# A decoder layer on one core: the quarter of the down projection that is multiplied directly moves from the end to both ends, and GpSimd issues the loads of the hidden operands

## The chip, the core and the metric

The kernel runs on one core of a Trainium2 chip as one launch. The metric is the device time of one execution in microseconds; the median of three runs of the kernel before is 2515.79 us (2514.77 to 2517.98).

## What is computed

Eight sequences of 100 tokens, model width 1024, go through a post-norm decoder layer: decayed linear attention, attention over a context of 722 tokens and the sequence itself, and a gated feed-forward block. Each is added to its input and normalised over the width. Only the last block matters here:

```python
gate = jnp.einsum('bsd,hd->bsh', x, w_gate)      # 4096 hidden rows
up = jnp.einsum('bsd,hd->bsh', x, w_up)
gated = jax.nn.silu(gate) * up
y = jnp.einsum('bsh,dh->bsd', gated, w_down)     # the down projection
out = _layernorm(x + y)
```

All of it is float32.

## The kernel before

**Numbers in two parts.** TensorE multiplies a fast 32-bit type, so every operand is split into a high part (ScalarE casts it, `split2`, L67) and a low rest (VectorE subtracts, L68). A product is three matmuls (`mm3`, L86 to L88): high by high, high by low, low by high. Activations lie transposed, width on the 128 partitions and tokens along the free side, in two halves of N = 400 tokens.

**Seven products instead of eight.** A unit of gate, up or down is a two by two block product. `seven` (L342 to L406) does it with seven products of 12 matmuls (128x128 weights by 128x400) instead of eight: four weight blocks a11 to a22 are loaded as two raw tiles `wst` (`load_raw`, three buffers, SP queue), VectorE makes three mixed blocks of them (L375 to L378), ScalarE and VectorE split the mixed and the raw blocks into `w` (four buffers) and `wd` (one buffer), and the products use seven operands b11, b21, t2, t3, t1, t4, b22 that hold blocks of the activations and their differences. `in_turn` (L408) interleaves neighbouring units by product, and a scheduler with its own model of time then fixes the order of the instructions on every engine and queue. Each engine works strictly in that order.

**Gate and up.** There are 16 units of 256 hidden rows. `combine` (L859 to L879) turns the product of gate and up of one unit into the operands of the down projection and stores them in device memory: for a seven-product quarter seven operands with their rests in `hd` (four stores, 1400, 200, 400 and 800 KB), for the direct quarter the four blocks alone in `h3d` (two stores of 800 KB). One quarter is four units. Tiles `r`, `t` and `h` of `combine` have one buffer each, so the next unit writes them only when the stores of the one before have landed.

**Down.** The hidden rows are summed in four quarters. Quarters 0, 1 and 2 are done by `seven`: four units each, whose products are added by VectorE straight to the rows `y` of the result (L360, L369). Quarter 3 is done directly: `proj` (L100) makes one product of 24 matmuls for each of the eight 128-wide blocks m of the result and for each half of the tokens, and VectorE adds it to `y` (L994). So the direct quarter comes last, first all eight blocks of half 0 and then all eight of half 1. Its eight split weight tiles `ws` are made once in half 0 and kept for half 1 (four in `w`, four in operand slots that are free by then).

**Operand slots.** Ten slots of 1600 KB take the operands of the down projection in rotation: `f`, three `z`, four `big` (which until the end of the up projection hold the operands of gate and up) and two `h` (which lie where pools of gate and up lay). `load_chunk` (L918) loads the seven operands of a quarter, one DMA of 1600 KB each. These DMAs are issued by SP, on the same queue as the weights `wst` and the stores, where the scheduler has put them. So a weight load stands behind an operand load that waits for its slot, and behind its bytes.

**The end.** Half 0 is normalised (`norm_root`, `scaled`) while half 1 is multiplied. Half 1 uses `norm_early`: the mean over the first six blocks (L294) is taken off before the last two are there, then `norm_more` and `norm_late` correct it. `scaled` (L271) and the stores of the result (L274) end the kernel.

Of the kernel before, what the change touches and what calls it, by code (L numbers as in the profile page):

```python
# [11 lines left out]
ALU = mybir.AluOpType  # L12
# [8 lines left out]
KT = D // P  # L21
QT = KT // 2
# [11 lines left out]
UNITS = NHID // 2  # L34
# [5 lines left out]
def decoder_layer(ctx, tc, xT, cT, w1, wo1, w2, wo2, wc, w3, wd, gw, qw, kw, trig, dec, mask, out):  # L40
    nc = tc.nc

    def sbuf(name, bufs, side=None):
        return tc.tile_pool(name=name, bufs=bufs, side=side, reuse_waits="tile")
# [11 lines left out]
    def f32(ap):  # L56
        return ap.bitcast(F32)
# [38 lines left out]
    def acc_tag():  # L96
        turn[0] += 1
        return "as"[turn[0] % 2]

    def proj(w, z, n=N, tag="a"):  # L100
        acc = bank(tag)[:, :n]
        for k in range(KT):
            t = z[k // QT]
            mmw(acc, w, k, t[:, 0, k % QT, :n], t[:, 1, k % QT, :n], k == 0, k == KT - 1)
        return acc
# [54 lines left out]
    hd = dr.tile([QT - 1, 7, P, 2, QT, N], FR, name="hd")  # L160
    h3d = dr.tile([4, P, 2, QT, N], FR, name="h3d")
# [129 lines left out]
    def norm_early(y, s1, p, first=KT - 1):  # L291
        n = y.shape[2]
        mean = bank("s")[:, :n]
        nc.tensor.matmul(mean, onem7, s1, start=True, stop=True)  # L294
        f = (KT - 1) / first
        for m in range(first):
            nc.vector.scalar_tensor_tensor(y[:, m], mean, -f, y[:, m], ALU.mult, ALU.add)
        var, delta = bank("v")[:, :n], bank("s")[:, :n]
        nc.tensor.matmul(var, onem, squares(y, p, range(first)), start=True, stop=False, skip_group_check=True)
        return mean, var, f, delta, first  # L300
# [26 lines left out]
    def load_raw(src):  # L327
        st = wp.tile([P, KT * P], F32, tag="wst", name="wst", bufs=3)
        if isinstance(src, list):
            for i, s in enumerate(src):  # L330
                nc.sync.dma_start(out=st[:, i * H:(i + 1) * H].rearrange("p (u c) -> p u c", u=QT), in_=s)
        else:
            nc.sync.dma_start(out=st, in_=src)
        return st

    def w_split(src, w=None):
        if w is None:
            w = wp.tile([P, 2, KT * P], FR, tag="w", name="w", bufs=4)
        split(w, src)
        return w  # L340
# [67 lines left out]
    def in_turn(units):  # L408

        at = sorted((7 * i + 2 * j, i) for i in range(len(units)) for j in range(-1, 7))  # L410
        started = {}
        for _, i in at:
            make, then = units[i]
            if i not in started:
                started[i] = make()
            try:
                next(started[i])
            except StopIteration:
                then()


    with sbuf("l1", 2) as p:
# [106 lines left out]
        for blk in range(2):  # L529
            w = load_w(w1[0, 2 + blk])  # L530
# [12 lines left out]
        def unit(h, i, then):  # L543
            c = {}
            return (lambda: seven(p, w1[h, i], w1[h, i + 1], zb, "ass", temp, c.__setitem__),
                    lambda: then(h, [(hb, c[name]) for hb, name in zip(HB, C)]))
# [75 lines left out]
    early = []  # L622
    with sbuf("l2", 2) as p:
        for kv in range(NKV):
            for i0, i1 in ((0, 4), (4, 6)) if kv == 0 else ((0, 2), (2, 4), (4, 6)):
                if (kv, i0) == (0, 4):
                    load_context(0)
                ws = [load_w(w2[kv, i]) for i in range(i0, i1)]
# [5 lines left out]
                for half in range(2):  # L634
                    bs = slice(half * NB, (half + 1) * NB)
                    for i in range(i0, i1):
                        acc = proj(ws[i - i0], z1[half], tag=acc_tag())
# [139 lines left out]

    fp = ctx.enter_context(sbuf("fp", 1, "right"))  # L780
    z2p = ctx.enter_context(sbuf("z2", 1, "right"))
    zb = {}
# [76 lines left out]
    def combine(u, r):  # L859
        h = ff.tile([P, 7, N], FR, tag="h", name="h")  # L860
        q, j = u // QT, u % QT
        if q == QT - 1:
            split2(h[:, 0:4], r, r)
            nc.sync.dma_start(out=f32(h3d[:, :, 0, j]).rearrange("c p n -> p c n"), in_=f32(h[:, 0:4]))
            nc.sync.dma_start(out=f32(h3d[:, :, 1, j]).rearrange("c p n -> p c n"), in_=r)
            return
        t = ff.tile([P, 4, N], F32, tag="t", name="t")
        pairs = r.rearrange("p (i x) n -> p i x n", x=2)
        nc.vector.tensor_tensor(t[:, 0:2], pairs[:, :, 1], r[:, 0:2], ALU.subtract)
        nc.vector.tensor_tensor(t[:, 2], r[:, 3], t[:, 0], ALU.subtract)  # L870
        nc.vector.tensor_tensor(t[:, 3], r[:, 2], t[:, 2], ALU.subtract)
        split2(h[:, 3:7], t, t)
        split2(h[:, 1:3], r[:, 2:4], r[:, 2:4])
        split2(h[:, 0], r[:, 0], r[:, 0])
        to = lambda a, b, l: f32(hd[q, a:b, :, l, j]).rearrange("c p n -> p c n")
        nc.sync.dma_start(out=to(0, 7, 0), in_=f32(h))
        nc.sync.dma_start(out=to(0, 1, 1), in_=r[:, 0:1])
        nc.sync.dma_start(out=to(1, 3, 1), in_=r[:, 2:4])
        nc.sync.dma_start(out=to(3, 7, 1), in_=t)  # L879
# [13 lines left out]

    def after_up(u):
        if u == QT:
            load_chunk(0, down_order[:1])
        elif u == UNITS - 2:
            load_y(fp)
        elif u == UNITS - 1:
            ffpool.__exit__(None, None, None)  # L900
            sppool.__exit__(None, None, None)
            load_y(ctx.enter_context(sbuf("yy", 1)))
            pools.append(sbuf("hk", 1))
            hk = pools[0].__enter__()
            hk_slots.append(lambda: hk.tile([P, 2, QT, N], FR, tag="h", name="h", bufs=2))
            slots[0:0] = hk_slots * 2


    slots = [f_tile, z_tile, z_tile] + [lambda: big([P, 2, QT, N])] * 4 + [z_tile]
# [4 lines left out]
    def next_slot():  # L914
        slots.append(slots.pop(0))
        return slots[-1]()

    def load_chunk(q, names):  # L918
        for name in names:
            chunk[q, name] = next_slot()  # L920
            nc.sync.dma_start(out=f32(chunk[q, name]), in_=f32(hd[q, ORDER7.index(name)]))

    def load_y(pool):
        for _ in range(2):
# [15 lines left out]
    def down_w(q, m):  # L940


        w = wd[q * QT:(q + 1) * QT, m // QT].rearrange("u p c -> p u c")
        c = m % QT * 2 * P
        return [w[:, :, c + i * P:c + (i + 1) * P] for i in range(2)]

    def down_unit(q, m):
        def make():
            if m == 0 and q == 0:
                load_chunk(0, down_order[1:])  # L950
            z = {name: chunk[q, name] for name in ORDER7}
            into = {"c%d%d" % (i + 1, j + 1): y2[m // 2][:, i, j * N:(j + 1) * N] for i in range(2) for j in range(2)}
            return seven(fp, down_w(q, m), down_w(q, m + 1), z, "ass", into=into)

        def then():
            if m != 2:
                return
            if q < QT - 2:
                load_chunk(q + 1, down_order)
            else:  # L960
                for half in range(2):
                    z3.append([next_slot() for _ in range(2)])
                    for i in range(2):
                        nc.sync.dma_start(out=f32(z3[half][i]), in_=f32(h3d[2 * i + half]))
        return make, then

    for name in C:
        gated_block(0, name, None)
    z3 = []
    in_turn([unit(u) for u in range(1, UNITS) for unit in (gate_unit, up_unit)]  # L970
            + [down_unit(q, m) for q in range(QT - 1) for m in range(0, KT, 2)])
    pools[0].__exit__(None, None, None)
    slots = [slot for slot in slots if slot not in hk_slots]


    ln_exp()
    with sbuf("ln3", 2, "right") as lnp:
        ws = []
        for half in range(2):
            y = rows(half)  # L980
            s1 = lnp.tile([P, N], F32, tag="s1", name="s1", bufs=2)
            early = None
            for m in range(KT):
                if half == 0:
                    w = None
                    if m >= QT:
                        w = next_slot().rearrange("p l k n -> p l (k n)")[:, :, :KT * P]
                    ws.append(w_split(load_raw(down_w(QT - 1, m)), w))
                elif m == KT - 2:
                    early = norm_early(y, s1, lnp, m)  # L990
                acc = proj(ws[m], z3[half], tag=acc_tag())
                if early:
                    nc.vector.scalar_tensor_tensor(y[:, m], early[0], -early[2], y[:, m], ALU.mult, ALU.add)
                nc.vector.tensor_tensor(y[:, m], y[:, m], acc, ALU.add)  # L994
                if early:
                    norm_more(y, early, lnp, m)
                else:
                    add_up(s1, y, m)
            dst = lambda m, half=half: out[:, m, half * N:(half + 1) * N]
            if half == 0:  # L1000
                scaled(y, norm_root(y, s1, lnp), dst)
            else:
                norm_late(y, early, lnp, dst)
# [71 lines left out]
```

## Time and profile before

| what | value |
|---|---|
| median of three runs | 2515.79 us |
| the profiled execution: its own time | 2517.7 us |
| its span, first to last instruction | 2515.9 us |
| TensorE busy | 2465.4 us, 98 % of the span |
| VectorE busy | 1992.2 us, 79 % |
| ScalarE busy | 1343.5 us, 53 % |
| GpSimd busy | 481.2 us, 19 %; nothing after 1700 us |
| mean granted TensorE clock | 0.993 |
| moved by DMA | 433.96 MB, mean 172 GB/s |

The span is cut by instructions, so the profiled execution's own time is 1.8 us above it, and it is 1.9 us above the median of the runs. TensorE is the engine to look at: matmuls of 128x400 follow each other every 0.18 us, and time is lost where they don't. "Idle" of another engine costs nothing by itself. Times in the views are microseconds from the start of the span; the down projection runs from about 2220 us to the end.

### The profile page before, as it was taken

The page shows a single profiled execution, that of the slowest core. Times are in us where ns is not written, and L with a number is a line of the kernel's source. Part 1 is how long each engine was busy: PE and PEld are TensorE (multiplying, and loading weights), DVE is VectorE, ACT ScalarE, POOL GpSimd, SP SyncE. Part 2 cuts the span into 40 slices and gives each one's busy share as a digit, 9 for nine tenths or more (in the row PEclk, how much of TensorE's full clock was granted, in tenths as well). Part 3 has the DMA queues.
Part 4 walks back from the last instruction along what each step waited for, and adds up shares of the span by engine and source line. Part 5 has one row for each costly group of instructions (what it writes and reads, how often), then busy time and mean ns, then how long its engine had stood idle before and what let it go on. Part 6 is the DMA issues. An engine that isn't in the chain of part 4 may idle for free.

```text
span 2515.9 us, 37158 instructions
## 1 busy us (share of the span) xinstructions
PE 2465.4 (98%) x14036; PEld 2442.0 (97%) x14036; DVE 1992.2 (79%) x3110; ACT 1343.5 (53%) x2264; POOL 481.2 (19%) x234
## 2 busy tenths in 40 slices
PE   8999999999899999999999999999999999999997
PEld 8999999999899999999999999999999999998997
DVE  7678876568989798899999999866987777666656
ACT  6667676335767565556566566533544544432221
POOL 0111111002645334433433433100000000000000
PEclk9999999999999999999999999999999999999999
DMA  7334445774444654554554554574455445388731
GB/s 240 110 110 127 136 144 187 239 266 148 144 152 133 207 175 142 178 166 151 169 176 144 166 192 135 189 273 152 145 181 192 159 160 167 127 302 311 250 102 53
DMA packets 224450, 433.96 MB, mean 172 GB/s; under 512 B 47338, under 2 KB 168042, under 8 KB 211854
## 3 DMA queue, kind: packets, MB, share of 16 engines
q1 hardware_dynamic: 223118, 427.39, 50.7%
q0 software_dynamic: 1152, 4.19, 1.1%
q8 instruction: 110, 1.80, 0.3%
q14 instruction: 70, 0.57, 0.1%
HBM read 322.18 MB, written 109.35 MB: 172 GB/s over the span
## 4 chain that ended last, share of the span: by engine, by line
PE 89%; DVE 6%; ACT 1%; DMA 1%; issue 1%; SPq 0%; DVEq 0%; ACTq 0%
PE a L88 18%; PE a L86 18%; PE a L87 18%; PE s L88 9%; PE s L87 9%; PE s L86 9%; PE v L88 2%; PE v L86 2%; PE v L87 2%; PE s L491 1%; PE s L688 1%; DVE r L120 1%; DVE r L119 1%; PE s L148 1%; DMA tp<-in_xT 1%
## 5 line engine op out<-in xcount | busy, mean ns | idle before, releaser
L86 PE MATMUL a<-big,w 128*128 128x400 f32 (+2 forms) x1808 | 611.4, 339 | 11.7 <-ACT big L67 7.4
L87 PE MATMUL a<-big,w 128*128 128x400 f32 (+2 forms) x1808 | 611.1, 338 | 0.0
L88 PE MATMUL a<-big,w 128*128 128x400 f32 (+2 forms) x1808 | 609.7, 338 | 0.0
L67 ACT CAST w<-wst 128x1024 fp32r<-128x1024 f32 (+1 forms) x231 | 239.2, 1038 | 389.4 <-PE s L88 130.7
L68 DVE TENSOR_TENSOR w<-wst,w 128x1024 fp32r<-128x1024 f32 (+1 forms) x231 | 281.0, 1218 | 117.0 <-ACT w L67 115.1
L86 PEld LDWEIGHTS a<-big,w 128*128 128x128 f32 x1808 | 341.3, 189 | 13.3 <-ACT big L67 7.7
L87 PEld LDWEIGHTS a<-big,w 128*128 128x128 f32 x1808 | 342.0, 189 | 1.3 <-DVE big L68 0.3
L88 PEld LDWEIGHTS a<-big,w 128*128 128x128 f32 x1808 | 342.0, 189 | 0.9 <-DVE w L68 0.2
L86 PE MATMUL s<-big,w 128*128 128x400 f32 x664 | 230.6, 347 | 0.1
L87 PE MATMUL s<-big,w 128*128 128x400 f32 x664 | 229.2, 345 | 0.0
L88 PE MATMUL s<-big,w 128*128 128x400 f32 x664 | 229.1, 346 | 0.0
L125 POOL PARTITION_ALL_REDUCE ss<-sq x56 | 161.1, 2881 | 336.3 <-DMA zd<-y 167.0
L605 POOL PARTITION_ALL_REDUCE kss<-ksq x64 | 173.2, 2706 | 116.4 <-ACT ksq L604 115.7
L86 PE MATMUL a<-z,w 128*128 128x400 f32 x488 | 168.6, 346 | 8.0 <-ACT r L118 4.3
L88 PE MATMUL a<-z,w 128*128 128x400 f32 x488 | 169.4, 348 | 0.7 <-DVE w L68 0.7
L87 PE MATMUL a<-z,w 128*128 128x400 f32 x488 | 169.4, 347 | 0.0
L87 PE MATMUL s<-z,w 128*128 128x400 f32 x400 | 139.1, 348 | 2.4 <-DVE z L68 2.4
L86 PE MATMUL s<-z,w 128*128 128x400 f32 x400 | 139.9, 350 | 0.0
L88 PE MATMUL s<-z,w 128*128 128x400 f32 x400 | 139.4, 348 | 0.0
L722 ACT ACTIVATE s<-s,rk 128x400 f32<-128x400 f32 x160 | 87.7, 591 | 91.9 <-DVE sm L742 65.5
L86 PEld LDWEIGHTS s<-big,w 128*128 128x128 f32 x664 | 124.6, 188 | 1.4 <-ACT w L67 0.4
L87 PEld LDWEIGHTS s<-big,w 128*128 128x128 f32 x664 | 124.6, 188 | 1.1
(330 smaller groups left out, 5650.9 us busy)
## 6 DMA issues: line engine op xcount, KB each, us to landing
wst<-in_w SPq DMA_DIRECT2D x135, 512.0 KB
w<-wcd SPq DMA_DIRECT2D x64, 1024.0 KB
wst<-in_wo SPq DMA_DIRECT2D x64, 512.0 KB
hd<-h SPq DMA_DIRECT2D x12, 1400.0 KB
wst<-in_wd SPq DMA_DIRECT2D x64, 256.0 KB
big<-o1d SPq DMA_DIRECT2D x16, 800.0 KB
qd<-d SPq DMA_DIRECT2D x32, 400.0 KB
q<-qd SPq DMA_DIRECT2D x32, 400.0 KB
```

Source lines behind the costliest of these rows:

```text
L67: nc.scalar.copy(hi, src)
L68: nc.vector.tensor_tensor(lo, src, f32(hi), ALU.subtract)
L86: nc.tensor.matmul(acc, lh, rh, start=start, stop=False, skip_group_check=chain)
L87: nc.tensor.matmul(acc, lh, rl, start=False, stop=False, skip_group_check=chain)
L88: nc.tensor.matmul(acc, ll, rh, start=False, stop=stop, skip_group_check=chain)
L119: nc.vector.scalar_tensor_tensor(q, ss, eps, q, ALU.add, ALU.mult)
L120: nc.vector.scalar_tensor_tensor(q, q, 3.0, r, ALU.subtract, ALU.mult)
L125: nc.gpsimd.partition_all_reduce(y, x, P, op)
L148: nc.tensor.transpose(tr[0:T, b * P:(b + 1) * P], vt[:, b * T:(b + 1) * T], ident)
L491: nc.tensor.matmul(bt(o)[:, b], vv[:, b * P:(b + 1) * P], pf[:, b], start=True, stop=True)
L605: nc.gpsimd.partition_all_reduce(ss[:, at], sq[:, at], P, RED.add)
L722: nc.scalar.activation(sc, sp, AF.Copy, scale=rk[:, c:c + 1])
```

## The change

- The direct quarter is now quarter 0, the first that gate and up produce. `combine` stores units 0 to 3 to `h3d` and units 4 to 15 to `hd` (index q - 1).
- Half 0 of the direct quarter is multiplied right after the last up unit: eight products of 24 matmuls, each added to `y`. It needs two operand tiles; the first is loaded after unit 4, the second when its slot is free. During these eight products the seven operands of quarter 1 are loaded, one load put into the program before each.
- Then follow quarters 1, 2 and 3 by `seven`, with twelve units in one `in_turn` as before, but separate from gate and up.
- Half 1 of the direct quarter comes last. Its weights are loaded and split again, since the first split is not kept (eight more loads of 512 KB, eight more casts, eight more subtractions).
- Half 0 is normalised while half 1 of the direct quarter is multiplied.
- All 25 loads of down operands, 21 by `load_chunk` and four of `h3d`, 1600 KB each, are now issued by GpSimd, on its own queue; before all of them were SP's.
- The order of the slots differs: the two `h` slots come in ahead of the last one.

```diff
 def combine(u, r):
-        if q == QT - 1:
+        if q == 0:
...
-        to = lambda a, b, l: f32(hd[q, a:b, :, l, j]).rearrange("c p n -> p c n")
+        to = lambda a, b, l: f32(hd[q - 1, a:b, :, l, j]).rearrange("c p n -> p c n")
...
         if u == QT:
-            load_chunk(0, down_order[:1])
+            load_direct(0, 1)
...
-            slots[0:0] = hk_slots * 2
+            slots[-1:-1] = hk_slots * 2
...
-            nc.sync.dma_start(out=f32(chunk[q, name]), in_=f32(hd[q, ORDER7.index(name)]))
+            nc.gpsimd.dma_start(out=f32(chunk[q, name]), in_=f32(hd[q - 1, ORDER7.index(name)]))
+
+    def load_direct(half, blocks=2):
+
+        for i in range(len(z3[half]), blocks):
+            z3[half].append(next_slot())
+            nc.gpsimd.dma_start(out=f32(z3[half][i]), in_=f32(h3d[2 * i + half]))
...
+            if m == 2:
+                if q < QT - 1:
+                    load_chunk(q + 1, down_order)
+                else:
+                    load_direct(1)
...
-    in_turn([unit(u) for u in range(1, UNITS) for unit in (gate_unit, up_unit)]
-            + [down_unit(q, m) for q in range(QT - 1) for m in range(0, KT, 2)])
+    z3 = [[], []]
+    in_turn([unit(u) for u in range(1, UNITS) for unit in (gate_unit, up_unit)])
+
+    def direct(half, m, w=None):
+        return proj(w_split(load_raw(down_w(0, m)), w), z3[half], tag=acc_tag())
+
+    load_direct(0)
+    for m in range(KT):
+        load_chunk(1, down_order[m:m + 1])
+        y = rows(0)
+        nc.vector.tensor_tensor(y[:, m], y[:, m], direct(0, m), ALU.add)
+    in_turn([down_unit(q, m) for q in range(1, QT) for m in range(0, KT, 2)])
...
             for m in range(KT):
-                if half == 0:
+                if half == 1:
+                    if m == KT - 2:
+                        early = norm_early(y, s1, lnp, m)
+                        f = early[2]
                     w = None
                     if m >= QT:
                         w = next_slot().rearrange("p l k n -> p l (k n)")[:, :, :KT * P]
-                    ws.append(w_split(load_raw(down_w(QT - 1, m)), w))
-                elif m == KT - 2:
-                    early = norm_early(y, s1, lnp, m)
-                acc = proj(ws[m], z3[half], tag=acc_tag())
-                if early:
-                    nc.vector.scalar_tensor_tensor(y[:, m], early[0], -early[2], y[:, m], ALU.mult, ALU.add)
-                nc.vector.tensor_tensor(y[:, m], y[:, m], acc, ALU.add)
+                    acc = direct(half, m, w)
+                    if early:
+                        nc.vector.scalar_tensor_tensor(y[:, m], early[0], -f, y[:, m], ALU.mult, ALU.add)
+                    nc.vector.tensor_tensor(y[:, m], y[:, m], acc, ALU.add)
```

More of the change, by code (lines that the diff above doesn't have):

```diff
@@ L948, in make @@
         def make():
-            if m == 0 and q == 0:
-                load_chunk(0, down_order[1:])
             z = {name: chunk[q, name] for name in ORDER7}
@@ L955, in then @@
         def then():
[L956 to L964, printed above, removed]
+            if m == 2:
[3 more added lines that the diff above has]
+                    load_direct(1)
         return make, then
@@ L968, in decoder_layer @@
         gated_block(0, name, None)
-    z3 = []
-    in_turn([unit(u) for u in range(1, UNITS) for unit in (gate_unit, up_unit)]
-            + [down_unit(q, m) for q in range(QT - 1) for m in range(0, KT, 2)])
+    z3 = [[], []]
[8 more added lines that the diff above has]
+    in_turn([down_unit(q, m) for q in range(1, QT) for m in range(0, KT, 2)])
     pools[0].__exit__(None, None, None)
@@ L977, in decoder_layer @@
     with sbuf("ln3", 2, "right") as lnp:
-        ws = []
         for half in range(2):
```

## The prediction

> **What bounds the kernel now.** I read the busy shares, the windows by stage, the waits of TensorE, the chain that ended last, then VectorE's timeline and the DMA packets at the places that these name. TensorE is busy 98 % of the span, so only stretches with fewer matmuls than its pace hold anything to win. Windows of 50 us of the down projection, columns: TensorE busy and matmuls in brackets, then weight loads, VectorE, ScalarE, GpSimd, granted clock, DMA share, GB/s:
>
> ```profile
> 2200.00:2250.00 50.00, 50.00 (x276) 50.00 (x275) 35.79 (x49) 19.21 (x24) 0.00 (x0) 1.00 0.80 295
> 2250.00:2300.00 50.00, 48.95 (x263) 47.25 (x263) 31.06 (x46) 11.02 (x13) 0.00 (x0) 1.00 0.94 330
> 2300.00:2350.00 50.00, 46.81 (x242) 45.98 (x241) 31.46 (x46) 10.69 (x12) 0.00 (x0) 0.93 0.62 217
> 2350.00:2400.00 50.00, 50.00 (x276) 50.00 (x275) 35.11 (x50) 12.30 (x13) 0.00 (x0) 1.00 0.76 271
> 2400.00:2450.00 50.00, 50.00 (x277) 50.00 (x276) 26.24 (x36) 12.34 (x12) 0.00 (x0) 1.00 0.35 107
> ```
>
> Full pace is 0.1825 us a matmul, 274 in 50 us. 11 are missing in the second window (2.0 us) and 32 in the third (5.9 us). These **7.9 us** are all that the change can win before 2450 us; the up units in front show no gap. The second place, windows of 4 us and the chain there (start, length, work):
>
> ```profile
> 2314.00:2318.00 4.00, 2.27 (x13) 1.94 (x11) 2.23 (x4) 0.00 (x0) 0.00 (x0) 1.00 0.68 283
> 2318.00:2322.00 4.00, 2.54 (x7) 2.08 (x8) 3.93 (x6) 3.46 (x4) 0.00 (x0) 0.57 0.02 6
> 2322.00:2326.00 4.00, 4.00 (x15) 3.97 (x14) 2.95 (x4) 0.00 (x0) 0.00 (x0) 0.58 0.87 255
> ```
>
> ```profile
> 2316.09 0.20 PE a L88
> 2316.34 0.46 issue
> 2316.80 0.69 DVE ws L375
> 2317.51 0.70 DVE wst L376
> 2318.36 1.05 ACT w L67
> 2319.46 0.70 PE s L86
> 2320.16 0.33 PE s L87
> ```
>
> TensorE ends a product, VectorE adds it to y (the "issue" is that add, L369, 0.57 us), and only then mixes the next unit's weights (L375, L376), ScalarE casts, TensorE goes on: 3.1 us idle. Then matmuls come every 0.33 us, as the clock is at half for 6.8 us. The raw weights were there: by the packets, the four loads issued from 2299.21 to 2308.1 us moved from 2309 to 2314, behind operand loads of 12,800-byte packets in the same SP queue. What came last was the **order on VectorE**: the scheduler had put the add in front of the mixing, because it took the weights to be late. The first place (2282 us) is the same thing, milder: 0.7 us, then some 1.4 us.
>
> **The change part by part.**
>
> *Matmuls.* The built programs have the same 13,610 rows on TensorE: 0.
>
> *SP freed of operand loads.* The weights no longer wait behind slots and 12,800-byte packets. But SP's waits are not what TensorE waits for last; the order on VectorE is. So I read that order in the changed program, and count for each place where TensorE needs a fresh `w` how many matmuls lie between the last product that VectorE must first add and this need, times 0.1825, against add, mix, cast.
> - The first place is gone: the tightest other transition of quarters 1 to 3 keeps 0.5 us. **-2.0 us.**
> - The second is back in another place: where half 0 of the direct quarter ends and quarter 1 begins, the order on VectorE is L360, L369, then L375 to L378, and TensorE's rows there (2 matmuls of t3, 2 of the next unit's b11, 2 of b21, 2 of t2, then t3's lows) are those of 2319.46 us line by line. Zero matmuls lie between. Idle 0.57 + 0.70 + 0.71 + 1.05 and hand-overs = 3.1 us, and half a clock for 3.4 to 6.8 us (the trace has both lengths: 3.4 us after the idles near 608 and 714 us, 6.8 here), 1.7 to 3 us lost. I take the same as before, 5.9: **0**, at best -1.3.
>
> *The end.* As before, half 0 is normalised under the eight direct products of half 1, but its variance matmul L283 stands later among them: in before 64 matmul rows lie between L283 and the mean of half 1 (L294), in after 44. The work between is, from before: L283 at 2479.76 to L119 at 2482.95 = 3.2, L119 0.6, L120 0.5, one add to y 0.5, eight L271 3.9, one L254 0.6 = 9.3 us. 44 x 0.1825 + 0.36 for L283 = 8.4 us. **+0.9 us** of wait on TensorE; in before the 64 rows left 2 us to spare. After L294 both programs have 24 matmuls and the same chain, so the end itself is 0.
>
> *The second split of eight weight tiles*: 8 x 1.05 us on ScalarE, 8 x 1.22 = 9.8 us on VectorE, 8 x 512 KB. In the last 72 us VectorE is busy 38.85 us, ScalarE 13.42, the DMA engines 12 %. The casts lie ahead of need by 3 us or more in both orders: 0. Without that cover they would be part of the wait for L283 (3.5 us spare, counted in the same way).
>
> *combine* of units 12 to 15 gets the seven-operand form and units 0 to 3 the short one: same work elsewhere, 0 on engines; its stores (2800 KB a unit instead of 1600) now lie just where the operand loads begin, see the rival.
>
> *GpSimd's issues.* No plain load by GpSimd is in the trace. Nearest rows: its eight accumulating stores took 0.89 to 1.18 us of issue and 6.4 us to land 512 KB (packets of 4096 bytes 328 ns; SP's loads of this size 159 ns), and SP's loads of 1600 KB are eight packets of 482 ns on each of 16 engines, 3.9 us. Lower end 3.9 us a load; upper end 328/159 of that, 8 us (of the 6.4 us only 8 x 0.328 = 2.6 are transfer, the rest is latency that overlaps); I take 3.9, the same shape and direction. Counting from the first slot that comes free (b11 of the last up unit; up and gate are interleaved, so slots come free every 2 to 4 us), the loads are issued at 2, 7, 11, 15, 18, 22 and 24 us, the seventh operand of quarter 1 after the last unit's stores at some 40; TensorE needs the first at 24, the next at 57, 59, 61. Even at 8 us each they land in time: 0. GpSimd does nothing else after 1700 us, so nothing queues behind its waits.
>
> Sum: -2.0 + 0 + 0.9 = **-1.1 us**. On the profiled execution (span 2515.9, 1.8 around it, own time 2517.7) that is 2516.6; the median of the runs lies 1.9 lower, and 2515.8 - 1.1 = **2514.7 us**.
>
> **The rivals.**
>
> *A. Weights starved in the first half of the direct quarter (slower).* It takes 512 KB of weights every 24 x 0.1825 = 4.4 us, a seven-product unit 1024 KB in 15.3 us. At the same time seven operands (27 us of all engines) and two units' stores (7.3 us each: 1792 packets of 67 ns on 16 engines) move, in a stretch whose DMA share in before was already 1.04 (2214 to 2282 us). What counts is how an engine divides itself between GpSimd's queue and SP's. Before shows it once: from 41.0 to 43.0 us, beside an accumulating store of GpSimd, 68 of its 4096-byte packets started and 57 of SP's 1600-byte ones; loads that SP issued at 39.3 landed at 45. That looks like one packet each in turn. With 12,800-byte packets at 482 ns, SP then gets 56 packets per engine in the 31 us of seven loads. The stores of unit 14 alone are 112 per engine; so they end near 39 us and the fourth direct weight tile near 41, needed at 31 to 35: 7 to 10 us idle, since `combine` of unit 15 also waits on VectorE for those stores. With half clock (1.7 to 3) that is +9 to +13, in sum +8 to +12: **2524 to 2528 us**. It decides if SP gets less than about half of the bytes then; at half the stores end near 18 us and the tile near 24, and nothing waits. Against it: GpSimd's packets in the row were twice slow, and the seven loads come one by one as slots open.
>
> The Trainium skill ("DMA: Bandwidth & Descriptors", Queues, rings and completion order) says that an engine goes round the queues packet by packet and that a packet is typically 9 to 17 descriptors. The row agrees with turns but not with so many small descriptors to a turn; by the page SP's 512-byte pieces would go many to one big one, the rival would fall and the sum stay at -1.1, by the row it can be +8 to +12.
>
> *B. Nothing is left of the stalls (faster).* If the weights mattered after all and the new place did not idle, 7.9 - 0.9 = 7.0 us would be won: **2508.8 us**. Against it stands VectorE's order in the program, which no DMA changes.
>
> *C. The change does not do what it says.* Moving SP's loads brings nothing, both stalls come back with full half clock, and the late mean adds 0.9: **2516.7 us**. For it: nothing in before shows TensorE waiting for an operand load.
>
> **How the numbers follow.** The forecast and C together (they differ by the first stall) 0.59, A 0.34, B 0.07. About 0.2 % (5 us) is what a measurement of this kernel can tell from no change: faster is below 2510.8, slower above 2520.8. The forecast and C lie inside with a little over either side; A lies above but for its mildest forms; B is below. Faster 0.08, same 0.57, slower 0.35. The range reaches from B to the upper end of A: 2509 to 2528; the likeliest case's own is 2512 to 2518.
>
> **What would show it.** Right: full pace (274 per 50 us) through the eight direct products; one idle of 3.1 us some 57 us after the last up unit's first product, ended by L375, L376 and a cast, and half clock behind it; none later; L294 waiting for L254 by about 1 us. Rival A shows as idle TensorE inside the direct products or the last up unit, with VectorE or ScalarE waiting for `wst` from the weights or for `hd` stores. B shows as no idle at the start of quarter 1. I am wrong too if GpSimd's loads land late enough that a matmul waits for an operand, or if its packets slow SP's at the later changes of quarter, where seven loads again come in 30 us.

## The result, and the profile after

The changed kernel takes 2551.5 us (median of 4 runs, 2550.7 to 2553.5), the kernel before 2516.4 in the same session: ratio 1.0137, 95 % interval 1.0125 to 1.0149. The forecast was 2514.7 us, its range ended at 2528. The profiled execution of the changed kernel has a span of 2549.3 us, 33.4 more than before's 2515.9.

The windows of 50 us that the prediction began with, now of the changed kernel (columns as there: TensorE busy and its matmuls, weight loads, VectorE, ScalarE, GpSimd, granted clock, DMA share, GB/s):

```profile
2200.00:2250.00 50.00, 36.27 (x187) 35.89 (x187) 23.59 (x32) 15.81 (x21) 3.52 (x7) 0.83 0.78 293
2250.00:2300.00 50.00, 40.09 (x212) 39.19 (x211) 23.20 (x30) 11.09 (x11) 2.39 (x5) 0.91 0.92 322
2300.00:2350.00 50.00, 50.00 (x272) 49.99 (x271) 36.48 (x53) 12.59 (x14) 1.61 (x3) 0.98 0.48 162
2350.00:2400.00 50.00, 43.81 (x227) 43.42 (x226) 26.81 (x39) 9.52 (x10) 2.15 (x4) 0.93 0.59 215
2400.00:2450.00 50.00, 46.95 (x249) 46.59 (x249) 30.59 (x45) 11.20 (x12) 3.23 (x6) 0.97 0.72 260
2450.00:2500.00 50.00, 50.00 (x275) 49.70 (x274) 34.65 (x49) 14.32 (x16) 0.00 (x0) 1.00 0.30 85
```

At 274 matmuls to 50 us, 87, 62, 2, 47 and 25 are missing: 223 x 0.1825 = 40.7 us, against 7.9 before. That is +32.8 us; with 0.7 at the mean of half 1 it makes the 33.4 of the span but for 0.1. So the whole loss lies here: two thirds before 2300 us, around the direct half and the change to quarter 1, and a third at the later changes of quarter, where the forecast had none.

What TensorE waited for after 2100 us (engine, operand and line, what released it: us in total, times, longest):

```profile
PE a L86 <- DVE s L369: 13.7, 1, 13.7
PE s L86 <- ACT w L67: 9.9, 1, 9.9
PE s L86 <- DVE y L360: 9.2, 2, 6.2
...
PE s L294 <- DVE s L254: 0.7, 1, 0.7
```

Four idle places: 13.7 us near 2231, 9.9 near 2287, 6.2 near 2372 and 3.0 near 2440 (the third line holds the last two), each with a stretch at half clock in or behind it. No matmul waits for an operand load. The engines named are not the cause; they were waiting themselves. The waits of the other engines from 2200 to 2320 us:

```profile
DVE r L853 <- DMA hd<-r: 22.1, 1, 22.1
ACT h L67 <- DMA hd<-h: 21.2, 1, 21.2
ACT w L67 <- DMA wst<-in_wd: 20.7, 4, 9.5
...
DVE ws L375 <- DMA wst<-in_wd: 6.6, 1, 6.6
```

L853 is the multiplication of `gated_block` that writes `r` of unit 15. `r` has one buffer, and the store of unit 14 still reads it: that store was issued at 2214.4 and landed at 2242.7, 28.3 us later. VectorE stands there, the additions that empty TensorE's accumulators stand behind it in its queue, and TensorE stops. At the other three places it is raw weights. The chain at the second (start, length, work):

```profile
2276.50 17.93 DMA wst<-in_wd
...
2294.52 0.70 DVE ws L375
...
2295.25 0.70 DVE wst L376
...
2296.10 1.05 ACT w L67
...
2297.19 0.70 PE s L86
```

Its tail, L375, L376 and the cast, is the one shown of before at 2316 us, as forecast; but in front of it now stands a load of 256 KB that took 17.9 us. The loads at the third and fourth place took 21.2 and 18.0 us (issued 2351.2 and 2421.4). What the DMA engines did meanwhile, in windows of 4 us at the first place:

```profile
2228.00:2232.00 4.00, 3.33 (x19) 2.99 (x17) 0.00 (x0) 0.00 (x0) 0.38 (x1) 1.00 0.98 413
2232.00:2236.00 4.00, 0.00 (x0) 0.00 (x0) 0.00 (x0) 0.00 (x0) 0.16 (x1) 0.66 1.02 430
2236.00:2240.00 4.00, 0.00 (x0) 0.00 (x0) 0.00 (x0) 0.00 (x0) 0.00 (x0) 0.50 1.03 432
```

They were full (share 1.02, 430 GB/s) while TensorE, VectorE and ScalarE computed nothing. The packets of the trace say with what; a packet is one entry of its DMA records, and a piece is a run of bytes that lies together in memory. Packets that started in 4 us, over 16 engines:

```
changed kernel      GpSimd's queue       SP's queue
2232 to 2236 us     118 of 12,800 bytes  131 of 1600 (stores)
2236 to 2240 us     119 of 12,800        129 of 1600
2364 to 2368 us     128 of 12,800         97 of 512 (weights)
```

About one packet each in turn. A packet of GpSimd's takes 480 ns, one of SP's 27 or 67 ns. From 2232 to 2240 us the most frequent distance between two starts is 535 to 540 ns in either queue, about one packet of each; turns of several packets would show 480 and 67. So SP's queue gets 3 to 12 % of the bytes while an operand load is in flight.

**The theory** after this look: the turns starve SP's stores and weights, at every change of quarter. **The rivals**: the order itself (with the direct half in front, more bytes are wanted than the engines move, whoever issues); a software queue that is favoured whatever its packets are.

### The profile page after: what moved, and what is told of

It reads as the page before. It is cut to its first block, busy times and chain, and to the rows that moved or that the text cites. A ratio compares the mean times of both kernels' runs of the same rounds, so it can differ in the third digit from the quotient of the medians.

```text
span 2549.3 us, 37248 instructions
## 1 busy us (share of the span) xinstructions
PE 2470.2 (97%) x14036; PEld 2446.5 (96%) x14036; DVE 2004.2 (79%) x3118; ACT 1352.1 (53%) x2272; POOL 495.3 (19%) x259
## 4 chain that ended last, share of the span: by engine, by line
PE 84%; DVE 8%; DMA 5%; issue 1%; ACT 1%; SPq 1%; DVEq 0%; ACTq 0%
PE a L86 17%; PE a L88 17%; PE a L87 17%; PE s L88 9%; PE s L87 9%; PE s L86 9%; DMA wst<-in_wd 2%; PE v L88 2%; PE v L86 2%; PE v L87 2%; DMA hd<-r 1%; PE s L491 1%; DVE r L120 1%; DVE w L68 1%; PE s L688 1%
## 5 line engine op out<-in xcount | busy, mean ns | idle before, releaser
L86 PE MATMUL a<-big,w 128*128 128x400 f32 (+2 forms) x1808 | 610.5, 339 | 10.1 <-ACT big L67 6.5
L67 ACT CAST w<-wst 128x1024 fp32r<-128x1024 f32 (+1 forms) x239 | 247.6, 1038 | 414.1 <-PE a L88 145.1
L68 DVE TENSOR_TENSOR w<-wst,w 128x1024 fp32r<-128x1024 f32 (+1 forms) x239 | 291.3, 1221 | 132.5 <-ACT w L67 131.3
L86 PEld LDWEIGHTS a<-big,w 128*128 128x128 f32 x1808 | 340.8, 189 | 11.5 <-ACT big L67 7.2
L86 PE MATMUL s<-big,w 128*128 128x400 f32 x664 | 232.1, 350 | 16.1 <-ACT w L67 9.9
L86 PE MATMUL a<-z,w 128*128 128x400 f32 x504 | 175.5, 348 | 21.7 <-DVE s L369 13.7
L88 PE MATMUL a<-z,w 128*128 128x400 f32 x504 | 175.9, 349 | 0.7 <-DVE w L68 0.7
L87 PE MATMUL a<-z,w 128*128 128x400 f32 x504 | 175.7, 349 | 0.0
L86 PE MATMUL s<-z,w 128*128 128x400 f32 x416 | 146.2, 351 | 3.0 <-DVE y L360 3.0
L87 PE MATMUL s<-z,w 128*128 128x400 f32 x416 | 145.6, 350 | 2.4 <-DVE z L68 2.4
L88 PE MATMUL s<-z,w 128*128 128x400 f32 x416 | 145.6, 350 | 0.0
L86 PEld LDWEIGHTS s<-big,w 128*128 128x128 f32 x664 | 125.7, 189 | 17.8 <-ACT w L67 10.2
```

The lines of the kernel that those rows point to most:

```text
L67: nc.scalar.copy(hi, src)
L68: nc.vector.tensor_tensor(lo, src, f32(hi), ALU.subtract)
L86: nc.tensor.matmul(acc, lh, rh, start=start, stop=False, skip_group_check=chain)
L87: nc.tensor.matmul(acc, lh, rl, start=False, stop=False, skip_group_check=chain)
L88: nc.tensor.matmul(acc, ll, rh, start=False, stop=stop, skip_group_check=chain)
```

## The experiments

Times are medians; the kernel before ran beside them at 2517.0 us (experiments 1, 2, 4 and 5), 2516.5 (3, 6, 7 and 9) and 2515.2 (8 and 10 to 12). Ratios are to it, with 95 % intervals.

**1. The new order with the old queue.** In `load_chunk` and `load_direct`, for all 25 operand loads:

```
-            nc.gpsimd.dma_start(out=f32(...
+            nc.sync.dma_start(out=f32(...
```

> The changed kernel with its 23 operand loads issued by SyncE instead of GpSimd; TensorE's, VectorE's and ScalarE's instruction order is the same as in the changed kernel, row by row. Theory (in the changed kernel a DMA engine takes one packet from GpSimd's queue and one from SP's in turn, so SP's 512- and 1600-byte packets wait behind 12,800-byte ones): with one queue the turns are gone; the idle of 13.7, 6.2 and 3.0 us go, the stall of VectorE's order at the change from the direct products to quarter 1 stays: 2510 to 2522 us. Rival 'order' (the direct quarter in front asks too much of the DMA engines, whoever issues): still above 2540 us, with TensorE idle inside the direct products near 2231 us.

Measured: 2530.7 us, 1.0054 (1.0037 to 1.0070). Neither range holds it: 20.8 us below the changed kernel, but 13.7 above before. The windows show that the later places are gone and the front is not:

```profile
2200.00:2250.00 50.00, 50.00 (x275) 49.69 (x274) 33.14 (x43) 19.34 (x24) 0.00 (x0) 1.00 0.81 297
2250.00:2300.00 50.00, 35.35 (x152) 32.89 (x151) 16.39 (x21) 7.65 (x8) 0.00 (x0) 0.80 0.98 338
2300.00:2350.00 50.00, 50.00 (x276) 50.00 (x276) 37.08 (x54) 13.34 (x15) 0.00 (x0) 1.00 0.55 195
2350.00:2400.00 50.00, 50.00 (x276) 50.00 (x275) 34.96 (x49) 12.71 (x14) 0.00 (x0) 1.00 0.67 225
```

The chain of waits of the same kernel (start, length, work):

```profile
2241.57 17.27 DMA wst<-in_wd
...
2266.51 5.16 DMA wst<-in_wd
2271.66 0.02 issue
2271.68 14.59 DMA wst<-in_wd
```

The weights are late, 17.3 and 14.6 us, with one queue only. So the theory was half of it: there are two causes. (The expectation says 23 loads; it is 25.)

**2. The old order with the new queue.** The kernel before, `sync` replaced by `gpsimd` in its operand loads:

> The kernel before with its operand loads issued by GpSimd, nothing else; order on TensorE, VectorE and ScalarE nearly that of before. Theory (packets in turn): the weights land 18 to 21 us after their issue at each change of quarter instead of 6 to 10, TensorE idles there three times: 2525 to 2550 us. Rival 'order': the queue makes nothing, 2512 to 2520 us.

Measured: 2540.0 us, 1.0089 (1.0074 to 1.0104; by the medians +23.0), as the theory said. Its windows lose matmuls at the first quarter and at each change:

```profile
2200.00:2250.00 50.00, 40.48 (x222) 40.14 (x220) 22.49 (x30) 14.55 (x20) 3.77 (x7) 0.92 0.80 304
2250.00:2300.00 50.00, 48.10 (x241) 45.42 (x240) 34.17 (x50) 12.63 (x14) 2.15 (x4) 0.94 0.68 240
2300.00:2350.00 50.00, 45.85 (x239) 44.48 (x238) 33.18 (x48) 10.82 (x12) 2.69 (x5) 0.97 0.72 248
2350.00:2400.00 50.00, 43.30 (x236) 42.95 (x235) 27.39 (x41) 10.14 (x11) 3.76 (x7) 0.96 0.73 278
```

Together 1 and 2 make a square: order alone +13.7, queue alone +23.0, both +34.5 (2551.5 to 2517.0), nearly the sum of 36.7.

**3. GpSimd only in front.** `load_chunk` with `(nc.gpsimd if q == 1 else nc.sync)`, `load_direct` with `(nc.sync if half else nc.gpsimd)`:

> The changed kernel with GpSimd issuing only the loads of the first direct half and of quarter 1; those of quarters 2 and 3 and of the last half are SyncE's. Order on TensorE, VectorE and ScalarE as in the changed kernel. Theory (packets in turn, at every change of quarter): the idle places near 2372 and 2440 us go, 47 and 25 missing matmuls or 13 us, the ones near 2231 and 2287 us stay: 2535 to 2542 us. Rival 'all of it is the burst at the direct quarter' (order alone): 2548 us or more.

Measured: 2530.6 us, 1.0059 (1.0044 to 1.0074): 20.9 below the changed kernel, the same as with no GpSimd load at all.

```profile
2200.00:2250.00 50.00, 35.42 (x185) 35.06 (x185) 23.67 (x32) 15.71 (x21) 3.78 (x7) 0.86 0.79 295
2250.00:2300.00 50.00, 46.81 (x249) 46.01 (x247) 26.68 (x35) 11.10 (x11) 0.54 (x1) 0.97 1.00 340
2300.00:2350.00 50.00, 50.00 (x276) 50.00 (x276) 36.83 (x53) 13.64 (x15) 0.00 (x0) 1.00 0.58 199
2350.00:2400.00 50.00, 50.00 (x276) 50.00 (x275) 35.17 (x51) 12.40 (x13) 0.00 (x0) 1.00 0.67 224
2400.00:2450.00 50.00, 50.00 (x276) 50.00 (x276) 35.34 (x51) 13.03 (x14) 0.00 (x0) 1.00 0.61 216
```

From 2250 us on it has 37, 4, 49 and 27 matmuls more than the changed kernel, 117 x 0.1825 = 21.4 us: the loads of quarters 2 and 3 and of the last half account for all of GpSimd's cost. The first three of them are issued before 2300 us, at 2268, 2281 and 2283, and lengthen the place near 2287. The expectation had put 13 us on them all, missed these, and its range was too high. In front, GpSimd only moves the loss: here TensorE is idle for 14.6 us at the store of unit 14, in experiment 1 it waits for late weights, and the time is the same.

**4. Weights in large pieces.** Only the layout of `wd` in memory and its load:

```
-        w = wd[q * QT:(q + 1) * QT, m // QT].rearrange("u p c -> p u c")
-        c = m % QT * 2 * P
-        return [w[:, :, c + i * P:c + (i + 1) * P] for i in range(2)]
+        return wd[q, m]
```

For each tile, one load of 128 pieces of 4096 bytes takes the place of two loads that have 1024 pieces of 512 bytes together.

> The changed kernel with the down projection's raw weights laid out so that one load of 512 KB is 4096-byte pieces instead of two loads of 512-byte pieces; stores stay at 1600 bytes, operand loads stay GpSimd's. Theory (packets in turn): a raw tile takes 8 turns of an engine instead of 64, so it lands in 5 to 7 us beside operand loads; the idle of 6.2 and 3.0 us and the late part of the one at the change to quarter 1 go, the 13.7 us at the stores of unit 14 stay, as does a stall of VectorE's order: 2530 to 2541 us. Rival 'order' (bytes decide): within 4 us of the changed kernel, 2547 to 2555 us.

Measured: 2535.5 us, 1.0071 (1.0056 to 1.0086). As expected of the turns: 16 us are back, and the windows from 2350 to 2450 us are full, the first of them:

```profile
2350.00:2400.00 50.00, 50.00 (x276) 50.00 (x275) 32.53 (x47) 11.69 (x13) 2.32 (x5) 1.00 0.60 227
```

From 2356 to 2360 us 110 packets of GpSimd's started and 86 of SP's, now of 4096 bytes. From 2200 to 2250 us there are still only 216 matmuls; the stores there are 1600 bytes as before, which fits, but was not tried apart in this run. The scheduler's order on VectorE came out different at the first quarter, so the 16 us need not be the pieces alone; experiment 9 has no such difference.

**5 and 6. Operand loads in small pieces.** First `hd` and `h3d` laid out as [2, QT, P, N] for each operand (loads of 1600-byte pieces), then `hd` as [QT, P, 2, 7, N] (stores of up to 11,200 bytes, loads of 1600):

> The changed kernel with hd and h3d laid out so that GpSimd's operand loads are made of 1600-byte pieces instead of 12,800-byte ones; same bytes, same queue, same order on every engine. Theory (packets in turn): SP's 1600-byte stores then get half of the engines and the 512-byte weight pieces one in two packets, in place of 4 to 11 % of the bytes; store of unit 14 lands within 15 us instead of 28.3, most of the 33 us go: 2514 to 2526 us. Rival 'the software queue is favoured whatever its packets are': SP's stores and weights still take 18 to 28 us, 2543 us or more. Rival 'order': no change, 2545 to 2555 us.

> The changed kernel with hd laid out so that the stores of combine are made of the large pieces (11,200, 6400, 3200, 1600 bytes for each partition) and the operand loads of small ones; same bytes, queues and order on the engines. Theory (packets in turn): SP's queue gets most of the bytes while the stores run, the stores of units 13 and 14 land in 5 to 12 us instead of 28, VectorE's wait of 22 us for them and TensorE's idle of 13.7 us near 2231 us go; the 512-byte weights still wait in turn afterwards: 2530 to 2543 us. Rival 'order' (bytes decide): 2547 us or more, the idle of TensorE only moved.

Measured: 2556.0 us, 1.0153 (1.0138 to 1.0168), and 2551.9, 1.0148 (1.0131 to 1.0165). The theory's ranges failed in both; the times lie where the rivals put them. The windows of the second:

```profile
2200.00:2250.00 50.00, 42.32 (x225) 41.96 (x224) 28.74 (x38) 16.64 (x22) 6.42 (x7) 0.93 0.80 295
2250.00:2300.00 50.00, 32.70 (x163) 31.22 (x162) 16.72 (x22) 9.54 (x10) 3.91 (x4) 0.85 0.94 319
...
2350.00:2400.00 50.00, 46.72 (x248) 46.35 (x247) 30.20 (x45) 10.36 (x12) 3.89 (x4) 0.97 0.70 230
```

The packets explain it. GpSimd's queue moved the 1600-byte pieces three to a packet, 4800 bytes in 190 to 210 ns; SP's went one by one:

```
                              GpSimd's queue   SP's queue
5: 2236 to 2240 us            255 of 4800      261 of 1600
6: 2232 to 2236 us            266 of 4800      269 of 512
5: 2368 to 2372 us            270 of 4800      286 of 512
```

So the turns hold for these sizes too; the rival of a software queue that gets more than its turns is ruled out, although its time came true. What failed was the size of the relief: joined, GpSimd's packets were three times what the expectation had, so a 512-byte packet against 4800 bytes still had a tenth of the bytes, and the weights stayed late. In front, the stores of experiment 6 did land sooner (VectorE waits 16.0 us for `r` instead of 22.1; 38 matmuls more before 2250 us), and 49 were lost in the next window: the idle only moved, as the rival said.

**7. Both layouts in the changed kernel** (4 and 6):

> Both layouts in the changed kernel: the down projection's raw weights in 4096-byte pieces (2535.5 us alone) and combine's stores in large pieces; GpSimd issues the operand loads, in small pieces now. In its order on VectorE no product that must be added lies right in front of weights that TensorE needs at once, so the 3.1 us stall at the change to quarter 1 isn't built in. Theory (packets in turn): SP's queue is never starved, so only what the DMA engines can't move in time is left: 2507 to 2522 us. Rival 'order' (the direct half in front asks for more bytes than the engines move, as with SyncE's loads at 2530.7 us): 2526 to 2536 us.

Measured: 2525.2 us, 1.0040 (1.0027 to 1.0053), between the two expectations at the rival's end. Nothing is lost before 2250 us or at the later changes, one window is left:

```profile
2200.00:2250.00 50.00, 50.00 (x276) 50.00 (x275) 33.81 (x44) 21.13 (x26) 6.42 (x7) 1.00 0.75 286
2250.00:2300.00 50.00, 40.41 (x196) 37.75 (x194) 19.41 (x27) 6.87 (x8) 3.91 (x4) 0.93 0.93 354
2300.00:2350.00 50.00, 49.86 (x274) 49.86 (x275) 38.13 (x55) 14.12 (x16) 5.83 (x6) 1.00 0.64 228
```

78 matmuls, 14.2 us, with the engines at 354 GB/s. From 2260 to 2264 us 181 packets of GpSimd's (4800 bytes) started and 166 of SP's (4096), so SP's queue had over 40 % of the bytes, and still its weight loads on the chain took 19 and 24 us from issue to landing. This is the cost of the order, with no starved queue. Of TensorE's waits from 2250 to 2301 us only two, 1.2 and 0.7 us, end with an add of VectorE; the others end with a cast or a split of late weights.

**8. The same with fewer bytes.** Quarter 1 leaves out the low parts of its operands: they are not loaded, and its products read the high parts in their place. So it does not compute the whole layer:

```
+            h = slice(0, 1 if q == 1 else 2)
+            nc.gpsimd.dma_start(out=f32(chunk[q, name][:, h]), in_=f32(hd[q - 1, :, :, h, ...
...
+        def __getitem__(self, key):
+            return self.t[key[0], 0, key[2]]
```

> The changed kernel with both layouts (2525.2 us) and the same add held, in which quarter 1 leaves out the low parts of its seven operands: they are not loaded and its products take the high parts twice. 5.7 MB less to load between 2212 and 2290 us; weights, stores and TensorE's work stay. Theory of the burst (the direct half in front needs 4 MB of weights in 35 us while the engines are full with operands and stores): the weights come sooner, most of the 14 us in 2250 to 2300 us go: 2508 to 2517 us. Rival (what delays the direct half isn't the engines' bytes but the chain of wst, split and w buffers): 2521 us or more.

Measured: 2512.5 us, 0.9988 (0.9979 to 0.9997); 12.7 us below experiment 7.

```profile
2250.00:2300.00 50.00, 47.85 (x252) 46.69 (x251) 29.58 (x41) 10.90 (x12) 3.68 (x4) 0.97 0.72 263
```

Weights and stores were the same, and TensorE made as many matmuls; the window gained 56 of them, 10.2 us. So the burst of bytes is the cause of most of what the order costs. (The held add of experiments 10 to 12 is in here as well; the 1.2 and 0.7 us above are gone too, so some 2 us of the gain can be its.) How much of the burst is the direct half's faster use of weights and how much the larger stores of the last units was not tried apart.

**9. The old order, GpSimd, large weight pieces:**

> The kernel before with GpSimd issuing the operand loads (2540.0 us alone) and the down projection's raw weights in 4096-byte pieces; order on the engines as before, with its stall of 5.9 us at the last change of quarter. Theory (packets in turn): at the later changes of quarter nothing starves; at the first one the 1600-byte stores still wait in turn, and the weights behind them in SP's queue: 2513 to 2526 us. Rival (a load of GpSimd delays SP's by something other than the size of SP's packets): 2534 us or more.

Measured: 2515.8 us, 1.0000 (0.9991 to 1.0010). Its windows, to hold against those of experiment 2:

```profile
2200.00:2250.00 50.00, 49.64 (x271) 48.75 (x270) 34.95 (x48) 19.25 (x25) 3.79 (x7) 1.00 0.83 328
2350.00:2400.00 50.00, 50.00 (x277) 50.00 (x276) 35.12 (x51) 12.02 (x14) 2.70 (x5) 1.00 0.65 257
```

The 23 us of experiment 2 are gone with nothing changed but the pieces of SP's weight loads: TensorE, VectorE and ScalarE run their instructions in the same order in both.

**10 to 12. The stalls of before.** L360, one line, in the kernel before; then with the weights of 4, then with GpSimd's loads too:

```
-                    nc.vector.tensor_tensor(into[name], acc, into[name], ALU.add)
+                    (tc.keep_in_program_order if name in ('c22',) else lambda i: i)(nc.vector.tensor_tensor(into[name], acc, into[name], ALU.add))
```

> The kernel before, with one add of each seven-product unit of the down projection (c22 in L360) held in program order on VectorE, which puts it behind the mixing of the next unit's weights; loads and queues unchanged. Theory of the prediction's first step (7.9 us of before are VectorE's order, its weights were there): both stalls go, 2507 to 2512 us. Rival (the weights come late at the change of quarter, behind operand loads in SP's queue): VectorE waits for them with the adds behind it, 2514 to 2526 us.

> The kernel before with the same add held and the raw down weights in 4096-byte pieces; SyncE issues all loads. If the order on VectorE was all: 2507 to 2512 us, as without the larger pieces. If the weights were late as well: 2 us or more below the kernel with the held add alone.

> The kernel before with the same add held, the raw down weights in 4096-byte pieces and the operand loads issued by GpSimd (2515.8 us without the held add). Theory (packets in turn; nothing starves once SP's weight packets are 4096 bytes; the rest was VectorE's order): 2507 to 2512 us. Rival (GpSimd's loads cost at the stores of the last up units whatever the weights): 2513 to 2520 us.

Measured: 2508.6 us, 0.9974 (0.9963 to 0.9984); 2508.0, 0.9968 (0.9955 to 0.9980); 2510.2, 0.9979 (0.9970 to 0.9988). The windows of the first:

```profile
2250.00:2300.00 50.00, 49.39 (x269) 48.36 (x268) 31.97 (x47) 10.90 (x12) 0.00 (x0) 1.00 1.01 359
2300.00:2350.00 50.00, 50.00 (x276) 50.00 (x275) 37.24 (x54) 12.79 (x14) 0.00 (x0) 1.00 0.69 237
```

The place at 2316 us is gone with the same loads on the same queue; with the held adds the scheduler moved others of VectorE's instructions, from 2242 us on. The three beat both kernels; among themselves their intervals overlap, so neither larger weight pieces nor GpSimd's queue brings anything that could be told on top. In 2250 to 2300 us they have 269, 276 and 251 matmuls: with GpSimd's loads some are still lost there.

## Why the prediction was wrong

- **7.9 us lost before, by VectorE's order and not by late weights: right in the main.** Holding one add of each unit gave 6.5 us (2515.2 to 2508.6; interval 4 to 9). At the first place 5 matmuls stay missing (0.9 us), and with large weight pieces and the same order on TensorE, VectorE and ScalarE none (276): that much was late weights.
- **The second place comes back at the change to quarter 1: right.** Where weights are less late it shows nearly by itself: TensorE's wait for the cast in experiment 3 is 3.2 us, forecast 3.1 (`PE s L86 <- ACT w L67: 3.2, 1, 3.2`). In the changed kernel the mixing and the cast are the tail of a 9.9 us wait; there they stand behind late weights, not behind the add.
- **L294: +0.9 us, measured 0.7: right.**
- **The first place gone, -2.0: not seen**, since larger losses lie there. Experiment 3 has 276 in each window from 2300 to 2450 us, which agrees.
- **"Even at 8 us each they land in time: 0": the step that failed.** It held GpSimd's loads only against TensorE's need for operands and gave nothing for what they do to SP's queue. No matmul waited for an operand. What they cost is what they did to SP's queue: 20.9 us (experiment 3). The row for it had been read, 68 packets to 57 at 41 us, and the rival worked out from it; but the forecast kept the zero, since the row's packets were slow and the loads come one by one as slots open. 19 of the last 24 came in three bursts, at most 4.4 us apart, and each of these took 8 to 12 us, so in a burst one was always in flight: from 2212 to 2244 us, 2337 to 2373 and 2407 to 2438. Their packets were not slow either, 480 ns.
- **Rival A had the mechanism and the first place, with too small a size.** Its arithmetic (the stores of unit 14 end late, and `combine` of unit 15 waits for them on VectorE) is what the trace shows near 2231 us, 13.7 us idle. But it priced the first half alone, at 8 to 12 us; the later changes of quarter stood only as a sentence on what would make the forecast wrong, without a price, so the range ended 23 us short of the time.
- **"SP's waits are not what TensorE waits for last": true of before, not of the new order.** The direct half asks for 512 KB every 4.4 us where a seven-product unit asks for 1024 KB in 15.3, at the moment when operands and stores already fill the engines. That demand was worked out in rival A, but only as something that an uneven queue would spoil. By itself it costs some 14 us: 13.7 over before with all loads on SP's queue (experiment 1), 14.2 of matmuls missing with two queues and large pieces (experiment 7). With the 20.9 that is the 35.1 us by which the changed kernel is slower, within 1.
- **Rivals B and C** fell: the new place does idle, and 2516.7 us needs a queue that costs nothing.
- On the **rule weighed there** (Trainium skill, "DMA: Bandwidth & Descriptors", Queues, rings and completion order): the turns packet by packet are what the traces show; a packet of 9 to 17 descriptors is not, if a piece is a descriptor. SP's packets were one piece, GpSimd's one of 12,800 or three of 1600 bytes. The measurement decides, and with it the rival stood.
- **Readings that change no term:** the 38.85 us of VectorE and the 12 % of the DMA engines are from 2428 to 2500 us, not from the last 72 us. The traces record 14,036 matmuls in either kernel, so the 0 for matmuls holds.

## What to carry to other kernels

When loads move to a second queue, don't only ask whether they land in time: count the packets. While two queues were busy here, each got one packet in turn, so their bytes went in the ratio of the packet sizes; make the pieces of what is urgent large before giving it a neighbour. And before work is moved to the front, add up the bytes that everything wants in that stretch: here it cost some 14 us whether one queue or two carried them. If a stall sits in the order of an engine's queue, mend the order there; here it took one line, and no change to a transfer.

## What had not been expected of the hardware

- GpSimd's plain load of 1600 KB cost 0.54 us of issue in 12,800-byte pieces and 0.92 in 1600-byte ones (6.42 us for seven), and its packets were not slow: 479 to 486 ns for 12,800 bytes, as SP's.
- Its queue joined three 1600-byte pieces to one packet of 4800; beside them SP's pieces of 512 and 1600 bytes went one to a packet.
- Small packets moved fewer bytes in a ns of their own time: 512 bytes in 27 ns are 19 bytes a ns, 4096 in 159 are 26, 12,800 in 480 are 27.
